# Expert matrices in halves, two experts' loads behind the transposes of gathered rows

## The chip, the cores and the metric

The kernel runs on one core of a Trainium2 chip. A core has a matrix engine (TensorE, PE in the profile), a vector engine (VectorE, DVE), a scalar engine (ScalarE, ACT), GpSimd (POOL) and a sync engine (SyncE, SP) that here only issues transfers. Each engine works through its own instructions in program order, and they wait for each other through semaphores. Transfers run on 16 DMA engines. The metric is the device time of one execution, in microseconds (us), lower is better.

## The reference

The input is x with 8 x 1024 tokens of 256 numbers. A first layer is an attention of each token over its own 16 x 64 numbers, followed by a residual and a normalisation. The second layer is an attention along the first axis (8 positions) for each of 1024 columns, and then a mixture of 8 experts, each with room for 1024 tokens:

```python
slot = jnp.where(keep, idx.astype(jnp.int32) * cap + loc, E * cap)
disp = jnp.zeros((E * cap, D), x.dtype).at[slot].set(xf, mode='drop')
h = jnp.einsum('ecd,edf->ecf', disp, w1) + b1[:, None, :]
y = (jnp.einsum('ecf,efd->ecd', h, w2) + b2[:, None, :]).reshape(E * cap, D)
out = jnp.where(keep[:, None], gate_val[:, None] * y[...], 0.0)
```

There is no nonlinearity between w1 and w2, so an expert is one 256 x 256 matrix w1·w2 and one bias row. The result is normalised, added to the second layer's input, and normalised again.

## The kernel before

**Phases A and B.** phase_a (L120) computes the first layer for 64 tiles of 128 tokens and writes them to DRAM. phase_b (L541) computes the second attention, the normalisation and the gate in 8 groups, and writes a row for each token to rows_d: the normalised value (256), the residual (256) and the gate (1). It also multiplies w1·w2 for experts 0 and 1 (EARLY = 2) and gathers every expert's bias row in acc.

**Phase C** (phase_c, L966) first turns the choice of experts into a list of tokens ordered by expert. VectorE computes each token's slot (L1036 to L1092); then in eight rounds it makes one-hot matrices is_low and is_high (L1111 to L1125), ScalarE makes `both` from is_high (L1127, L1129), and TensorE multiplies them into p_tok (L1139). From p_tok comes `token` (L1150), the indices for the gathers.

Meanwhile TensorE multiplies w1·w2 for experts 2 to 7. expert(e, fc) (L1001) does one of eight pieces of 128 hidden units, with four TensorE records in the trace; the products collect in one PSUM bank pw. After the last piece ScalarE copies the matrix to w12 (L1017), and then load(e + 3) (L995, transfers at L999) issues the next load on SP into one of three buffers. Loads for experts 2, 3 and 4 are issued at the start of the phase (L1027). The function some(k) takes the next k pieces from the list `pieces`; it is called with 8 before the slots are finished (L1052), once in each of the eight rounds (L1146), and with 8 after the token (L1151). So experts 2, 3 and 4 are done when the turns begin.

Then come turns r = -2 to 17 over sixteen batches q of Q = 4 tiles of 128 rows. The list `order` (L1294) is the order of issue in a turn, each entry with its offset of q to r. On GpSimd, gather (L1158) fetches a tile of rows by index, two turns ahead, and scatter (L1278) writes finished rows, two turns behind. turned (L1169) transposes a pair of tiles on TensorE (L1176), ScalarE copies it to xT (L1180), and product (L1183) multiplies it with the expert of the batch, e = q // 2 (L1187, L1197), one turn ahead. some(2) follows: two pieces of experts 5, 6 and 7 a turn, in turns -2 to 1, 2 to 5 and 6 to 9. blend (L1217), roots, scales, normed (L1261) and join (L1270) do both normalisations on VectorE and ScalarE. Expert 5 is needed from batch 10, so in turn 9.

Of the kernel before, what the change touches and what calls it, by code (L numbers as in the profile page):

```python
# [33 lines left out]
P = 128  # L34
# [7 lines left out]
E, FF = 8, 1024  # L42
FC = FF // P
CAP = L * N // E
RW = 2 * D + 1
EARLY = 2
# [4 lines left out]
def fused_kernel(ctx: ExitStack, tc: tile.TileContext, a: dict, out: bass.AP):  # L51
# [38 lines left out]
    nc.scalar.dma_start(keep["gain"], a["ln2_g"].partition_broadcast(P))  # L90
    phase_b(tc, a, ident, x1_d, rows_d, keep, norm_scalars)
    phase_c(tc, a, ident, rows_d, keep, out)


# [871 lines left out]
def phase_c(tc, a, ident, rows_d, keep, out):  # L966


    nc = tc.nc
# [3 lines left out]
    with (  # L973
# [18 lines left out]

        ex = {}

        def load(e):  # L995
            if e < E:
                ex[e] = [xp.tile([P, FC, D], FP, name=n) for n in ("w1", "w2")]
                for tile_, n in zip(ex[e], ("w1T", "w2")):
                    nc.sync.dma_start(tile_, a[n][e].rearrange("(c p) d -> p c d", p=P))  # L999

        def expert(e, fc):  # L1001

            w1, w2 = ex[e]
            if fc == 0:
                ex["w", e] = pw.tile([P, DC * D], FP, name="pw")
            ps = ex["w", e]
            for d in range(DC):
                nc.tensor.matmul(  # L1008
                    ps[:, d * D : (d + 1) * D],
                    w1[:, fc, d * P : (d + 1) * P],  # L1010
                    w2[:, fc, :],
                    start=fc == 0 and d == 0,
                    stop=fc == FC - 1,
                    skip_group_check=True,
                )
            if fc == FC - 1:
                nc.scalar.copy(keep["w12"][:, :, e, :], ps.rearrange("p (c d) -> p c d", c=DC))  # L1017
                load(e + 3)

        pieces = [(e, fc) for e in range(EARLY, E) for fc in range(FC)]  # L1020

        def some(k):
            for _ in range(k):
                if pieces:
                    expert(*pieces.pop(0))

        for e in range(EARLY, EARLY + 3):  # L1027
            load(e)
# [124 lines left out]
        st = {}  # L1153
# [15 lines left out]
        def turned(q, pair):  # L1169

            g = st["g", q]
            pt = pp.tile([P, 512], FP, name="ps")
            for i in range(2):
                for c in range(DC):
                    n = 2 * i + c
                    nc.tensor.transpose(  # L1176
                        pt[:, n * P : (n + 1) * P], g[:, 2 * pair + i, c * P : (c + 1) * P], ident
                    )
            xT = kp.tile([P, 4, P], FP, name="xT")
            nc.scalar.copy(xT, pt)  # L1180
            st["xT", q, pair] = xT

        def product(q, pair):  # L1183
            e = Q * q // ST
            xT = st["xT", q, pair]
            pr = pq.tile([P, 512], FP, name="pr")
            nc.tensor.matmul(  # L1187
                pr.rearrange("p (i d) -> p i d", i=2),
                keep["ones"],
                keep["acc"][:, e, None, :].to_broadcast([P, 2, D]),  # L1190
                start=True,
                stop=False,
                skip_group_check=True,
            )
            for i in range(2):
                for c in range(DC):
                    nc.tensor.matmul(  # L1197
                        pr[:, i * D : (i + 1) * D],
                        xT[:, 2 * i + c, :],
                        keep["w12"][:, c, e, :],  # L1200
                        start=False,
                        stop=c == DC - 1,
                        skip_group_check=True,
                    )
            st["pr", q, pair] = pr
# [72 lines left out]
        def scatter(q, i):  # L1278
# [18 lines left out]
            (gather, -2, 2),  # L1297
            (roots, None),
            (turned, -1, 0),
            (turned, -1, 1),  # L1300
            (product, -1, 0),
            (product, -1, 1),
            (some, None, 2),
            (blend, 0, 0),
            (scales, None),
# [62 lines left out]
```

## Time and profile before

| what | us |
|---|---|
| three timed runs: median (lowest to highest) | 5193.99 (5184.34 to 5194.05) |
| the profiled execution: its own time | 5145.15 |
| its span, from first to last instruction | 5143.4 |
| TensorE busy in it | 4903.2 (95%) |
| phase C, from the slots (L1036) to the end | about 4881 to 5143 |

The profile is of one execution. Its page gives busy time by engine, the span in 40 slices, the DMA queues, the chain of waits that ended last (each piece of work, followed back to what released it), and the costliest groups of instructions. The timeline lists instructions with start and length; in square brackets stands the idle time of the engine just before, and what ended it. "PEld" is the weight load of TensorE, "SPq" an instruction of SP's queue, "granted clock" the share of full speed that TensorE was allowed. A fp32 multiplication shows as two records. L is the line in the kernel.

Some steady rows of phase C: a turn takes about 10.4 us, a gather issue on GpSimd 0.97 us (64 of them), a scatter issue 1.04 us (64).

### The profile page before, as it was taken

How to read it: one execution, taken by the hardware profiler on the slowest of the kernel's cores; microseconds unless marked ns; L12 is line 12 of the kernel's file. 1: busy time of each engine (PE TensorE's matmuls, PEld its weight loads, DVE VectorE, ACT ScalarE, POOL GpSimd, SP SyncE). 2: the span in 40 equal slices, each digit the busy share in tenths (PEclk: the TensorE clock that was granted, in tenths of full speed). 3: DMA queues.
4: the chain of work that ended last, by engine and by line, in shares of the span. 5: the costliest groups of instructions: out<-in, count | busy, mean ns of one | idle time of the engine just before them, and what ended most of it. 6: DMA issues, size and time to landing. Idle time of an engine off the chain costs nothing. (4 is left out here: it accounts for less than half of the span.)

```text
span 5143.4 us, 189684 instructions
## 1 busy us (share of the span) xinstructions
PE 4903.2 (95%) x79688; PEld 3310.9 (64%) x79688; DVE 3070.0 (60%) x6088; ACT 3360.9 (65%) x4123; POOL 3374.4 (66%) x7014
## 2 busy tenths in 40 slices
PE   7999999999999999999999999999999997889675
PEld 4666666666666666666666666666666664566553
DVE  5665655666566666665666656666666563555467
ACT  5777777777777777777777777777777774444234
POOL 5667667677767767766776776776776764254436
PEclk9999999999999999999999999999999998999787
DMA  2222222222222222222222222222222222132253
GB/s 76 47 48 48 48 48 49 47 49 49 46 48 48 47 48 48 49 47 48 49 47 48 49 46 48 48 48 47 48 49 48 49 47 61 48 76 71 66 182 114
DMA packets 575308, 286.29 MB, mean 56 GB/s; under 512 B 394865, under 2 KB 526065, under 8 KB 574449
## 3 DMA queue, kind: packets, MB, share of 16 engines
q1 hardware_dynamic: 365970, 111.51, 10.9%
q0 software_dynamic: 204800, 159.82, 10.4%
q8 instruction: 623, 10.21, 0.8%
q10 hardware_dynamic: 3680, 2.83, 0.2%
q14 instruction: 235, 1.93, 0.1%
HBM read 72.31 MB, written 33.59 MB: 21 GB/s over the span
## 5 line engine op out<-in xcount | busy, mean ns | idle before, releaser
L359 ACT ACTIVATE e<-pair 128x1024 f32<-128x1024 f32 x3072 | 2977.4, 1021 | 1233.0 <-PE pair L343 1233.0
L403 POOL DMA_DIRECT2D nd<-S x4096 | 1952.9, 484 | 613.3 <-DVE S L393 420.9
L343 PE MATMUL pair<-R,L 32*128 32x128 f32 (+1 forms) x32768 | 1605.6, 322 | 2.0 <-POOL event L314 2.0
L393 DVE COPY S<-sum 128x512 f32<-128x512 f32 x1024 | 707.1, 691 | 1465.9 <-PE sum L382 1153.2
L343 PEld LDWEIGHTS pair<-R,L 32*128 32x128 f32 x32768 | 1271.3, 186 | 48.2 <-POOL event L314 2.6
L373 PE MATMUL sum<-e,V 128*32 128x256 f32 x16384 | 1284.9, 385 | 4.9 <-DVE S L393 4.9
L300 POOL DMA_DIRECT2D R<-qm x2048 | 973.8, 483 | 71.7 <-issue 39.2
L382 PE MATMUL sum<-e,V 128*32 128x128 f32 x16384 | 823.3, 273 | 0.0
L382 PEld LDWEIGHTS sum<-e,V 128*32 128x32 f32 x16384 | 532.8, 110 | 352.2 <-issue 0.9
L373 PEld LDWEIGHTS sum<-e,V 128*32 128x32 f32 x16384 | 406.3, 109 | 236.6 <-DVE qm L267 41.8
L331 PE MATMUL pair<-late,sel 32*128 32x256 bf16 (+1 forms) x6144 | 499.3, 313 | 9.6 <-ACT e L359 9.6
L254 DVE COPY V<-vT 32x128 f32<-32x128 f32 x2048 | 457.4, 223 | 28.1
L412 DVE RECIPROCAL att<-nd 128x256 f32<-128x256 f32 x256 | 447.4, 1748 | 8.0 <-DMA nd<-S 4.1
L331 PEld LDWEIGHTS <-sel 32*128 32x128 bf16 x6144 | 155.4, 91 | 460.4 <-issue 445.0
L314 POOL MEMSET event<- 1x1 f32 x256 | 22.8, 89 | 610.9 <-DMA R<-qm 416.4
L234 PEld LDWEIGHTS ps<-xT,wv 128*128 128x128 f32 x2048 | 238.2, 191 | 44.4 <-issue 41.8
L223 PE MATMUL ps<-wk,xT 128*128 128x512 f32 x512 | 255.3, 621 | 10.9 <-DMA wk<-in_Wk 10.1
L234 PE MATMUL ps<-xT,wv 128*128 128x128 f32 x2048 | 262.6, 281 | 1.6 <-DVE qm L267 0.8
L266 PE MATMUL ps<-wq,xT 128*128 128x512 f32 x512 | 255.7, 622 | 6.7 <-DVE k L224 6.7
L443 PE MATMUL ps<-wo,attT 128*128 128x256 f32 x1024 | 257.9, 395 | 0.7 <-ACT attT L426 0.7
L443 PEld LDWEIGHTS ps<-wo,attT 128*128 128x128 f32 x1024 | 186.1, 191 | 63.7 <-issue 41.8
L73 POOL TENSOR_SCALAR ve<-mv 128x1 f32<-128x1 f32 x128 | 37.9, 296 | 271.6 <-DVE mv L71 270.1
(191 smaller groups left out, 3856.0 us busy)
## 6 DMA issues: line engine op xcount, KB each, us to landing
R<-qm POOLq DMA_DIRECT2D x2048, 32.0 KB, 2.1
nd<-S POOLq DMA_DIRECT2D x4096, 16.0 KB, 1.9
L<-k SPq DMA_DIRECT2D x4088, 8.0 KB
rows_d<-yx SPq DMA_DIRECT2D x32, 512.0 KB
xT<-in_xT SPq DMA_DIRECT2D x64, 128.0 KB
xr<-in_x SPq DMA_DIRECT2D x64, 128.0 KB
x_d<-x1o SPq DMA_DIRECT2D x64, 128.0 KB
x<-x_d SPq DMA_DIRECT2D x8, 1024.0 KB
```

What stands on the lines that cost most here:

```text
L234: nc.tensor.matmul(ps[:, i * P : (i + 1) * P], w["v"][:, c, ch * P : (ch + 1) * P], xT_of[t][:, c, :], start=c == 0, stop=c == DC - 1,)
L254: nc.vector.tensor_copy(V[32 * aa : 32 * aa + 32, qd % 2, :, qd // 2, :, aa, 0:4], src[32 * qd : 32 * qd + 32, :, ww, :, aa, :],)
L300: moved.append((None, nc.gpsimd.dma_start(R[:, b, s, b, :], q[:, b, s, cols])))
L331: nc.tensor.matmul(bank[u].rearrange("p (n i) -> p n i", i=n)[:, :, 0:32], sel[pr].rearrange("p a j -> p (a j)"), late[pr, None, :].to_bro ...
L343: one = nc.tensor.matmul(bank[u][:, x * 4 * n : (x + 1) * 4 * n].rearrange("p (b i) -> p b i", i=n), Lt[pr, 2 * (h0 + h) + jb].rearrange(" ...
L359: nc.scalar.activation(e, pair[i], AF.Exp)
L373: nc.tensor.matmul(dst[32 * u : 32 * u + 32], Vs[ww][:, 0, h0 + h, u, :], e0[u // 2][:, u % 2, x * 256 : (x + 1) * 256].rearrange("p (b i) ...
L382: nc.tensor.matmul(dst[32 * u : 32 * u + 32, :, 32:], Vs[ww][:, 1, h0 + h, u, :], e1[u // 2][:, u % 2, h * 128 : (h + 1) * 128].rearrange( ...
L393: nc.vector.tensor_copy(S[:, :, 2 * which : 2 * which + 2, :].rearrange("p b h i -> p h b i"), ps.rearrange("p (h b i) -> p h b i", h=2, b=4),
L403: nc.gpsimd.dma_start(tok[:, b, s, h0 * C1 : (h0 + G) * C1], Sx[:, 4 if s else b, b, :])
L412: nc.vector.reciprocal(att[:, cols], nd[:, 1, cols])
L443: nc.tensor.matmul(ps[:, :D], attT[:, c, :], wo[:, c, :], start=c == 0, stop=c == HID // P - 1)
```

## The change

Loads come in halves: for each half of the hidden units first w1's four chunks, then w2's. For experts 2 to 5 all of an expert's halves are issued together, as before, in four transfers of 512 KB where there were two of 1 MB. Only expert 2's end still issues a load (that of expert 5). The loads of experts 6 and 7, which were issued at the end of experts 3 and 4, are cut into four half loads; load_behind, a new entry of `order` after the products, issues one of them in the turn of q = 0, 2, 4 and 6, and each waits for the last transpose of that batch.

```diff
-        def load(e):
-            if e < E:
+        wait = mybir.DependencyInfo(mybir.DependencyClass.Sync, mybir.DependencyReason.DATA)
+
+        def load(e, halves=(0, 1), behind=None):
+            if 0 in halves:
                 ex[e] = [xp.tile([P, FC, D], FP, name=n) for n in ("w1", "w2")]
-                for tile_, n in zip(ex[e], ("w1T", "w2")):
-                    nc.sync.dma_start(tile_, a[n][e].rearrange("(c p) d -> p c d", p=P))
+            for h in halves:
+                fs = slice(h * FC // 2, (h + 1) * FC // 2)
+                for w, n in zip(ex[e], ("w1T", "w2")):
+                    one = nc.sync.dma_start(w[:, fs, :], a[n][e].rearrange("(c p) d -> p c d", p=P)[:, fs, :])
+                    if behind is not None:
+                        tc.add_manual_dep(one.ins, behind.ins.name, wait, reason="transfers in turn with the rows")
+
+
+        halves = [(e, h) for e in range(EARLY + 4, E) for h in range(2)]
+
+        def load_behind(q):
+            if q % 2 == 0 and halves:
+                e, h = halves.pop(0)
+                load(e, (h,), st["turned", q])
...
-                load(e + 3)
+                if e == EARLY:
+                    load(e + 3)
...
-                    nc.tensor.transpose(
+                    last = nc.tensor.transpose(
...
             st["xT", q, pair] = xT
+            st["turned", q] = last
...
             (product, -1, 1),
+            (load_behind, -1),
             (some, None, 2),
```

## The prediction, on record before the result

> **What bounds the kernel now.** I read the page first. TensorE is busy for 95% of the span, nearly all of it in phases A and B, which the diff leaves alone. So only the last stretch can move: phase C, from about 4880 us to 5143.4. I then read the chain of waits from 4870 us.
>
> ```profile
> 4879.81 6.17 DMA rows_d<-gate
> 4886.32 0.37 SPq L999
> 4886.74 7.96 DMA w<-in_w
> 4894.70 0.38 issue
> 4895.08 10.00 PE pw L1008 x32
> 4905.58 0.73 ACT both L1127
> 4906.36 1.10 PE pr L1139 x8
> 4907.48 1.22 DVE is_low L991
> ...
> 4925.11 7.11 DMA g<-rows_d,token
> 4932.26 0.44 PE ps L1176 x2
> 4932.70 0.86 PE pr L1187 x2
> ```
>
> Each row is start, length, what. Two transfers stand in the chain. The first is the matrices of expert 2: TensorE cannot begin L1008 until both whole matrices are there, and VectorE's one-hot batches (L991) come behind that expert. The second is a gather of rows that lands 7.11 us after its issue began, with weights moving beside it. The timeline by instruction shows how much of each is waiting:
>
> ```profile
> 4889.60 0.63 PE L1051 MATMUL ps<-over,ones 128*128 128x64 f32 x2
> 4895.08 9.99 PE L1008 MATMUL pw<-w,w 128*128 128x256 f32 x32 [4.84 <-DMA w<-in_w]
> 4907.48 1.22 DVE L991 TENSOR_TENSOR is_low<-low,column 128x1024 bf16<-128x1024 f32 x1 [5.77 <-PE pr L1139]
> 4928.31 0.37 SPq L999 DMA_DIRECT2D w<-in_w1T  x1
> 4930.79 1.01 PE L1176 MATMUL ps<-ident,g 128*128 128x128 f32 x6
> 4931.36 0.20 PEld L1176 LDWEIGHTS ps<-ident,g 128*128 128x128 f32 x2 [0.20 <-DMA g<-rows_d,token]
> 4932.26 0.20 PEld L1176 LDWEIGHTS ps<-ident,g 128*128 128x128 f32 x2 [0.70 <-DMA g<-rows_d,token]
> ```
>
> TensorE waits 4.84 us for expert 2, VectorE 5.77 us for TensorE behind it. For the first gathered rows TensorE waits only 0.20 + 0.70 us, because up to 4930.8 it was still multiplying for experts 4 and 5. From 4932.3 to 4955.1 it runs without a wait.
>
> **Part 1: loads in halves.** load() now sends four transfers of 512 KB per expert where it sent two of 1 MB, the first halves of both matrices in front. This touches experts 2, 3, 4 (issued together) and 5, so eight more transfers in all. The first pieces of expert 2 need 1.05 MB instead of 2.10. The DMA view in steps of 1 us gives what had moved: 0.11 MB by 4888, 0.41 by 4889, 0.77 by 4890, 1.11 by 4891, 1.48 by 4892, and 2.44 by 4894.70, when the 2.10 MB were there (0.34 MB of the next transfer ran beside them). So 1.05 MB have moved at 4890.8 at the earliest; with the same 0.34 MB ahead (1.39 MB) it is 4891.76. I take the later, nearest to the measured landing, and add the 0.38 us issue row: L1008 starts at 4892.1 instead of 4895.08, 2.9 us earlier. The ends are 3.9 (nothing runs ahead) and 0 (TensorE still waits for the whole tile; the edit would then do nothing here). The second half should land near 4894.7 as now, while TensorE needs sixteen records first: no second wait.
>
> The 32 records take 10.0 us because the clock is half at first:
>
> ```profile
> 4895.00:4897.00 2.00, 1.92 (x5) 0.50 1.10 349
> 4899.00:4901.00 2.00, 2.00 (x6) 0.54 1.11 350
> 4901.00:4903.00 2.00, 2.00 (x11) 1.00 1.13 353
> ```
>
> Columns: stretch, length, TensorE busy (records), granted clock, DMA share, GB/s. The step to 1.00 comes about 5.8 us after the start. The same 32 records at full clock (4921.11) take 7.17 us, 0.224 each; so 13 ran slowly at 0.44 here. If 5.8 slow microseconds follow the new start too, the expert ends at 4892.1 + 10.0 = 4902.1, and the gain stays 2.9. [...] I keep 2.9, from the row.
>
> That gain reaches the token. VectorE has three one-hot batches ready at 4901.7 and then stands until 4907.48; at 4904.6 it still stands, so it takes up the whole 2.9. After it VectorE runs five rounds of 2.06 us with no wait, and the token, the first gather (4921.14) and TensorE's expert 4 (4921.11) follow together.
>
> [...] I cost the extra issues at nothing; what hides them is that the queue stays full, and SP (0.37 to 0.58 us for an issue that isn't held back) has nothing else to do.
>
> **Part 2: experts 6 and 7 move.** Removed: the four 1 MB loads issued at 4920.47, 4920.88, 4928.31 and 4928.73, which fill the DMA engines until about 4947, beside the first gathers. Those land in 7.1 us (median, 4920 to 4930) against 3.6 over the whole phase. At 3.6 the fourth gather, issued at 4925.11 - 2.9 = 4922.2, lands at 4925.8, before TensorE is free at 4930.8 - 2.9 = 4927.9. So the 0.20 + 0.70 = 0.9 us wait goes, and nothing more: what is late next is TensorE itself, with expert 4 in front of the transposes. Bounds: 0 if the gathers stay slow, and 0.9.
>
> Added: four pairs of half transfers (two DMA issues each), behind the last transposes of q = 0, 2, 4, 6. Only SP waits, and behind it on SP stand only the next halves and the end of the kernel. The buffers are long free (experts 3 and 4 are finished). Use comes late: expert 6's halves go out in turns r = -1 and 1 and are read from r = 2 and 4; expert 7's in 3 and 5, read from 6 and 8. A turn is 7.8 us at the start (TensorE) and 10.4 later, so each has over 15 us for some 4 to 7 us.
>
> Each half pair (1.05 MB at 350 GB/s, 3.0 us) meets gathers. In r = -1 there are over 10 us until those rows are turned; in r = 1 GpSimd has stopped gathering and stands until the first scatter (24.3 us idle). For r = 3 and 5, in the times of before:
>
> ```profile
> 4974.14 0.44 PE L1176 MATMUL ps<-ident,g 128*128 128x128 f32 x2 [0.98 <-DMA g<-rows_d,token]
> 4981.16 0.97 POOL L1162 DMA_INDIRECT g<-rows_d,token  x1 [0.30 <-issue]
> 4984.49 0.44 PE L1176 MATMUL ps<-ident,g 128*128 128x128 f32 x2 [1.74 <-DMA g<-rows_d,token]
> 5005.62 1.36 POOL L1283 DMA_INDIRECT out<-o,token  x1 [5.32 <-ACT o L1265]
> ```
>
> The half behind the transposes of 4974.14 moves from about 4976 to 4979. The gather that TensorE waits for next is issued at 4981.16, after it. In r = 5 the half moves from 4996.5 to 5000, and then GpSimd stands 5.3 us before the next deciding gather. I cost both at 0; the other end is 3.5 us each (7.1 - 3.6), 7.0 together, or 14.0 if all four cost it. A gain from them is excluded: nothing there waits for weights.
>
> **Sum.** -2.9 - 0.9 = -3.8 us: span 5143.4 becomes about 5139.6, the profiled time 5145.15 about 5141.3. The three timed runs are about 1% above the profiled one (median 5193.99), from work that the change leaves alone, so I carry the difference over: 5193.99 - 3.8 = 5190.2. The bounds of the mechanism: -5.0 (4.1 + 0.9) to +11.1 (-2.9 + 14.0, the 0.9 kept as it is). The three runs spread over 9.7 us, 0.19%; a difference within 0.2% (10.4 us) is about what measurement here cannot tell from none.
>
> **The rivals.**
> *No gain (0.20).* The halves help nothing, because the wait stays with whole tiles or six more transfers slow the first, and the early loads were covered anyway. For it: only 0.9 us of the gathers' slowness was ever waited for. Against it: L1008's pieces read only their own half. Between 0 and 0.9 saved: 5193.5.
> *More than the sum (0.13).* TensorE reaches full clock sooner and the quieter queues shorten the start-up beyond what I read, where GpSimd waits 24.3 us and VectorE 9.5. Against it: both hang on TensorE's unbroken work. A gain over 0.2% would need 10.4 us, twice my bound; 5182 would be such a result.
> *Slower (0.07).* The halves land on the loop gather, transposes, product, weights copy, norm, which has no slack in r = 5 (VectorE waits 5.4 us for it). Price 3.5 us per half. From the second half that costs it, the gain is gone; with all four, and the first gathers as slow as now, 5193.99 + 11.1 = 5205.1.
> *The sum as worked out (0.60):* 5190.2.
>
> **How the numbers follow.** Faster: 0.13 of the second rival, and 0.06 of the two cases near zero, since one of three runs sat 9.7 us under the median. Slower: 0.04 of the third rival (that with all four halves), and 0.02 for the spread. The rest, 0.75, is within 0.2%. The range is 5179 to 5198: below, the largest gain less the spread (5189 - 9.7); above, no gain and some 4 us, under half the spread.
>
> **What would show it.** Right: L1008's first wait shrinks from 4.84 to about 1.9 us, VectorE's 5.77 to about 2.9, the token and first gather come at about 4918.2, gathers there land in under 5 us, the 0.90 us before L1176 is gone, and the turns after it stay at 10.4 us. Wrong: L1008 starts at 4895 still; a second wait between its halves; gathers in r = 3 or 5 that hold TensorE beyond its 1.7 us; or a wait for w in a turn from r = 2 on. The prediction fails if phases A and B move by more than the 3.8 us at stake.

## The result and the profile after

| | median us (lowest to highest), runs | before, beside it | ratio, 95% interval |
|---|---|---|---|
| the change, first series | 5189.82 (5184.73 to 5195.04), 20 | 5191.43, 20 runs | 0.9997 [0.9991, 1.0004] |
| the change, second series | 5185.85 (5184.06 to 5191.25), 13 | 5190.71, 17 runs | 0.9992 [0.9984, 1.0001] |

The first series is the result: no difference that these runs can tell, between -4.7 and +2.1 us. The means of all runs of both series (33 and 37) differ by -2.7 us. Forecast were -3.8 us and 5190.2. Kernels are only compared with the kernel before on their own chip, because on one chip, used for three experiments below, the kernel before takes 5148.8 us.

The timeline of the changed kernel has these lines for the places shown before. (L1022 was L1008, L1154 was L1139, L1191 was L1176, L1195 and L1242 were L1180 and L1226, the copy to xT and the blend; L1213 was L1197, the product.)

```profile
4892.31 0.63 PE L1066 MATMUL ps<-over,ones 128*128 128x64 f32 x2
4894.69 9.95 PE L1022 MATMUL pw<-w,w 128*128 128x256 f32 x32 [1.75 <-DMA w<-in_w]
4907.06 1.23 DVE L991 TENSOR_TENSOR is_low<-low,column 128x1024 bf16<-128x1024 f32 x1 [2.64 <-PE pr L1154]
4930.15 1.01 PEld L1191 LDWEIGHTS ps<-ident,g 128*128 128x128 f32 x8
4930.37 1.04 PE L1191 MATMUL ps<-ident,g 128*128 128x128 f32 x8
4934.31 0.59 ACT L1195 COPY xT<-ps 128x512 f32<-128x512 f32 x1 [2.72 <-PE pr L1213]
4944.92 0.48 DVE L1242 SCALAR_TENSOR_TENSOR z<-pr,gate,g 128x256 f32<-128x256 f32 x1 [16.21 <-remote]
4947.95 1.07 ACT L1195 COPY xT<-ps 128x512 f32<-128x512 f32 x2 [13.05 <-remote]
```

The first three rows are the forecast's Part 1: 1.75 us of wait where 4.84 were, 2.64 where 5.77 were. The next two are its Part 2: eight transposes in one row and no wait for rows. The last three are new: ScalarE's second copy waits 2.72 us. VectorE's first blend waits 16 us for something with no recorded releaser ("remote"), ScalarE's next copy 13 us, though the transposes that it copies ended by 4939.5.

I call such waits holds. They are not the change's: the kernel before, profiled once more, has them too. The first two rows are its wait for expert 2, the third is its first blend, late as well, and the last two are held:

```profile
4898.03 9.96 PE L1008 MATMUL pw<-w,w 128*128 128x256 f32 x32 [4.40 <-DMA w<-in_w]
4910.41 1.23 DVE L991 TENSOR_TENSOR is_low<-low,column 128x1024 bf16<-128x1024 f32 x1 [5.30 <-PE pr L1139]
4943.84 0.48 DVE L1226 SCALAR_TENSOR_TENSOR z<-pr,gate,g 128x256 f32<-128x256 f32 x1 [8.22 <-PE ps L1176]
4950.93 0.48 DVE L1226 SCALAR_TENSOR_TENSOR z<-pr,gate,g 128x256 f32<-128x256 f32 x1 [4.88 <-remote]
4951.05 1.07 ACT L1180 COPY xT<-ps 128x512 f32<-128x512 f32 x2 [14.61 <-remote]
```

The chain of waits of phase C names them as "another core or an unknown queue", first in that second profile of before, then in the changed kernel:

```profile
4936.44 14.59 another core or an unknown queue
4996.07 8.21 another core or an unknown queue
5039.39 8.19 another core or an unknown queue
5066.13 8.29 another core or an unknown queue
5102.53 7.41 another core or an unknown queue
```

```profile
4934.89 13.03 another core or an unknown queue
4992.83 8.43 another core or an unknown queue
5036.20 8.33 another core or an unknown queue
5063.09 8.57 another core or an unknown queue
5099.46 8.29 another core or an unknown queue
```

The five sum to 46.7 us each time, and the chain of the first profile of before has no such row. Phase C (from the issue of the gate's store to the end) took 263.6 us in that first profile and 306.7 in the second: these 43 us are most of the 1% between the profiled execution and the timed runs that the prediction carried over.

Single executions of one program begin phase C up to 3 us apart (4879.81 and 4882.81 for before), so all profiles are compared from the issue of the gate's store. Times in us; the last three columns count from the first gather:

| profile | expert 2 starts | token | first gather | store to end | first blend | first scatter | end |
|---|---|---|---|---|---|---|---|
| before, first | 15.27 | 40.07 | 41.33 | 263.6 | 14.2 | 48.0 | 222.3 |
| before, again (holds) | 15.22 | 40.01 | 41.28 | 306.7 | 19.8 | 57.3 | 265.5 |
| changed (holds) | 12.40 | 37.17 | 38.45 | 305.0 | 24.2 | 57.4 | 266.6 |
| changed, again (holds) | 12.11 | 36.73 | 38.01 | 304.3 | 25.5 | 57.3 | 266.3 |
| halves alone | 12.46 | 37.23 | 38.49 | 260.8 | 14.3 | 48.2 | 222.3 |
| changed, gathers in turn | 12.73 | 37.10 | 38.36 | 259.7 | 13.3 | 47.1 | 221.3 |
| changed, expert 3 first | 18.56 | 41.99 | 43.25 | 266.4 | 13.3 | 47.1 | 223.1 |

What follows finds out which part of the gain arrives where.

### The profile page after: what moved, and what is told of

Read it like the earlier page. It is cut to its first block, busy times and chain, and to the rows that moved or that the text cites. A ratio compares the mean times of both kernels' runs of the same rounds, so it can differ in the third digit from the quotient of the medians.

```text
span 5187.3 us, 189704 instructions
## 1 busy us (share of the span) xinstructions
PE 4912.9 (95%) x79688; PEld 3314.9 (64%) x79688; DVE 3070.8 (59%) x6088; ACT 3360.4 (65%) x4123; POOL 3376.7 (65%) x7014
## 5 line engine op out<-in xcount | busy, mean ns | idle before, releaser
L443 PE MATMUL ps<-wo,attT 128*128 128x256 f32 x1024 | 257.8, 395 | 0.7 <-ACT attT L426 0.7
```

The costliest lines, as they stand in the source:

```text
L443: nc.tensor.matmul(ps[:, :D], attT[:, c, :], wo[:, c, :], start=c == 0, stop=c == HID // P - 1)
```

## The experiments

**Are the holds the change's doing?** The kernel before, unchanged.

> The kernel before, unchanged, profiled a second time. The profile of the change shows five waits of some 8 us in the turns (ScalarE's xT copy waits for transposes whose records ended long before), 40 us in all, and the profile of before shows none, though the two medians differ by 1.6 us. Theory A (the waits belong to the program as it usually runs): they stand in this profile too, its span is near 5189, and phase C from the gate's store to the end takes about 305 us. Theory B (the moved loads cause them, and the rest of the program is quicker by as much): none here, phase C about 264 us, and the span near 5189 only if phases A and B are 40 us longer than in the first profile.

5191.26 us, with the five holds shown above. They come without the moved loads too, and on three of the four chips that the experiments ran on; theory B falls.

**Phase C behind a short phase B.** Phase A is left out of three kernels, x is copied to its result, so that less noise lies ahead of phase C:

```diff
-    phase_a(tc, a, ident, x1_d, norm_scalars)
+    (x copied to x1_d, eight tiles of 128 rows at a time)
```

The third one has all loads in halves, but none moved:

```diff
-                if e == EARLY:
+                if e + 3 < E:
                     load(e + 3)
...
-            (load_behind, -1),
```

> The kernel before without phase A: x is copied to where the first layer's result would be, so the first layer is left out. Span some 590 to 650 us, in which a few us of phase C are 0.5% and can be timed. This is the base for the next two. Theory A: waits of some 8 us in the turns here too.

> The changed kernel, first layer left out as in the short kernel before. My sum: 3.8 us less than the short kernel before (5.0 at most, 1.6 at least). Rival 'no gain': within 1 us of it. Theory B (moved loads cause 8 us waits): 10 to 40 us more than it.

> Only the halves: experts 6 and 7 are loaded where they were, in halves like the others; first layer left out. My sum: 2.9 us less than the short kernel before, 0.9 more than the short changed kernel. Rival 'no gain': equal to the short kernel before. Theory B: quicker than the short changed kernel by 10 us or more.

Medians of five: 915.68, 915.74 and 915.24 us, each with runs 3.2 to 6.6 us apart; the time itself I had put far too low, because phase B and the copy take some 610 us. The medians tell nothing, the profiles do. Expert 2's row in the timeline of before, changed and halves alone (L1013 and L1027 are its line in these kernels):

```profile
630.82 10.14 PE L1013 MATMUL pw<-w,w 128*128 128x256 f32 x32 [5.07 <-DMA w<-in_w]
```

```profile
630.28 9.89 PE L1027 MATMUL pw<-w,w 128*128 128x256 f32 x32 [2.17 <-DMA w<-in_w]
```

```profile
629.75 10.12 PE L1027 MATMUL pw<-w,w 128*128 128x256 f32 x32 [1.57 <-DMA w<-in_w]
```

From the store, the token comes at 40.85, 37.71 and 37.33 us, the end at 300.1, 296.7 and 296.4, and from first gather to end it is 257.9, 257.7 and 257.8. All three have the holds. So in these single profiles the halves' 3.1 to 3.5 us reach the end of phase C whole (3.4 and 3.7 there), and the moved loads add and cost nothing (257.7 against 257.8).

**Phase C alone.** Phases A and B are left out; rows are copied from x, token p goes to expert p mod 8, and the matrices of experts 0 and 1 and the bias rows are zero. Four orders of loads: before, changed, halves alone (diff above), moved alone (experts 2 to 5 whole).

> Phase C of the kernel before alone: phases A and B are left out, the rows are copied from x, and token p of a tile goes to expert p mod 8, so every expert has its 1024 rows. With no work ahead that varies, a few us of phase C should be timed to about 1 us. This is the base for the next three. Span some 480 to 560 us; 8 us waits for transposes in the turns as in the repeated profile of before.

> Phase C of the changed kernel alone, the same parts left out. My sum: 3.8 us less than phase C of before alone (2.9 of it before the token, 0.9 at the first transposes). Rival 'no gain', now in a sharper form: the token comes 2.8 us earlier, as the profiles have it, but the turns give it back, so the two are within 1 us. Rival 'slower': the halves that move inside the turns cost up to 3.5 us each, and it is longer than with halves alone by 3 us or more.

> Phase C alone with the halves alone: experts 6 and 7 in halves at their old places. My sum: 2.9 us less than phase C of before alone, and 0.9 more than that of the change. If the turns give the gain back whatever the loads do: equal to before. If only the moved loads give it back: 2.9 us less than before and less than the change.

> Phase C alone with the move alone: experts 2 to 5 in whole matrices, 6 and 7 in halves behind the transposes. My sum: 0.9 us less than phase C of before alone. If moved loads cost something in the turns: longer than before by some us. The token's place is that of before in either case.

Medians of five: 478.77, 480.58, 479.51 and 481.25 us, each with runs 3.7 to 6.2 us apart. The halves can't help here: expert 2's weights came before they were wanted, and in all four its product starts 5.6 us after the same instruction of VectorE (the comparison `upto`). By the medians the moved loads would cost 1.1 us with halves (changed against halves alone) and 2.5 with whole matrices (moved alone against before); in the profiles, first gather to end is 258.6, 258.2, 259.7 and 260.1, so the moved loads there make -1.5 and +1.5. That is inconclusive, and it led me to expect 2 to 3 us in the next kernel, wrongly.

**The halves alone, in the whole kernel** (the second diff above). This and the next two ran together on the chip where the kernel before takes 5148.82 us (33 runs) and no profile has a hold.

> The whole kernel with one part of the change alone: every expert's matrices in halves, but the loads of experts 6 and 7 where they were before (behind an expert's product). Prediction's theory: the 2.9 us at L1008 are there (expert 2's product starts 12.4 us after the gate's store instead of 15.2, the token list at 37.2 instead of 40.0), and the time is 5188.5 (5191.4 less 2.9). Theory 2 (the moved loads cost some 2 to 3 us in the turns, as the timings of phase C alone had it): this kernel is 2 to 3 us below the changed one, 5187. Theory 3 (the turns swallow whatever the front gains): 5191, equal to before, with the token list still at 37.2. In the profile the stretch from the first gather to the end is the sum's test: 265.5 us in the repeated profile of before and 266.6 in the changed kernel; theory 2 wants 263 to 264 here, the others 265.5 to 266.6.

5145.98 us (13 runs), ratio 0.9995 [0.9987, 1.0004]. The prediction's theory holds for the halves: expert 2 at 12.46, token at 37.23, first gather to end 222.3 as in the first profile of before. Its timeline still has the waits for rows that Part 2 was to remove:

```profile
4894.22 9.95 PE L1022 MATMUL pw<-w,w 128*128 128x256 f32 x32 [1.76 <-DMA w<-in_w]
4906.59 1.23 DVE L991 TENSOR_TENSOR is_low<-low,column 128x1024 bf16<-128x1024 f32 x1 [2.65 <-PE pr L1154]
4930.61 0.20 PEld L1191 LDWEIGHTS ps<-ident,g 128*128 128x128 f32 x2 [0.35 <-DMA g<-rows_d,token]
4931.51 0.20 PEld L1191 LDWEIGHTS ps<-ident,g 128*128 128x128 f32 x2 [0.70 <-DMA g<-rows_d,token]
4934.57 0.48 DVE L1242 SCALAR_TENSOR_TENSOR z<-pr,gate,g 128x256 f32<-128x256 f32 x1 [2.82 <-PE pr L1213]
```

**Fewer gathers ahead of the first turn.** The first gathers of batches 2, 3 and 4 each wait for the first blend of the batch two earlier, so that 8 gathers and not 19 stand ahead of the first transposes. Cut to its core:

```diff
+            if i == 0 and 2 <= q <= 4:
+                tc.add_manual_dep(one.ins, st["first z", q - 2].ins.name, wait, reason="gathers in turn with the blends")
...
-            (gather, -2, 0),
-            (gather, -2, 1),
-            (gather, -2, 2),
...
             (blend, 0, 0),
+            (gather, -2, 0),
+            (gather, -2, 1),
+            (gather, -2, 2),
```

> The changed kernel, with the gathers of the batches 2 to 4 each waiting for the first blend (z) of the batch two earlier, so that 8 gathers stand ahead of the first transposes instead of 19. It tests what holds ScalarE's copy of the transposed rows (xT) in the first turn until 27.0 us after the first gather, in every profile but the first one of before, though the transposes' own records end by 19.3. Theory H (the release waits until the run of gathers has drained: 19 gathers end at 26.9): with 8 gathers, which drain by some 15 to 17, the third copy of xT comes at 16 to 19 us after the first gather instead of 27.0, the second batch's blend at 20 to 24 instead of 31.3, and if the later turns keep their rhythm the end comes 5 to 10 us earlier, 5180 to 5185. Theory I (the hold has nothing to do with the gathers: it is fixed in the program's order or in time): third xT still at 27, and the time 5190, or 2 to 6 us more, since a gather now is late for its transposes. Theory J (the hold goes, but the gathers held back land late): third xT early, end 5188 to 5195.

5143.26 us (13 runs), ratio 0.9992 [0.9983, 1.0000]. The test of theory H failed to come about: on this chip nothing is held, with 19 gathers ahead or with 8. But the kernel contains the whole change, and so shows it with no hold (L1193, L1197, L1244 and L1215 are here the transposes, the copy, the blend and the product):

```profile
4928.34 1.01 PEld L1193 LDWEIGHTS ps<-ident,g 128*128 128x128 f32 x8
4928.56 1.04 PE L1193 MATMUL ps<-ident,g 128*128 128x128 f32 x8
4929.19 1.07 ACT L1197 COPY xT<-ps 128x512 f32<-128x512 f32 x2 [2.52 <-PE ps L1193]
4932.22 0.48 DVE L1244 SCALAR_TENSOR_TENSOR z<-pr,gate,g 128x256 f32<-128x256 f32 x1 [5.37 <-PE pr L1215]
4936.97 1.07 ACT L1197 COPY xT<-ps 128x512 f32<-128x512 f32 x2 [6.70 <-PE ps L1193]
```

The waits for rows are gone, for the reason forecast: the gathers land sooner. The view of transfers from 4917 to 4931 (number of gathers issued, median us to landing) has first the halves alone, with weights still moving there, then this kernel:

```profile
g<-rows_d,token POOLq DMA_INDIRECT x9, 6.9
g<-rows_d,token POOLq DMA_INDIRECT x8, 3.8
```

In the next kernel, whose gathers stand in the old order, ten of them land in 3.9. The first blend comes 3.66 us after these transposes began, where the halves alone need 4.67 (from 4929.90 to 4934.57). The 1.0 us stays to the end: first scatter 47.1 against 48.2, end 221.3 against 222.3. Store to end is 259.7, 3.9 below the first profile of before. The slower gathers themselves add nothing: the next kernel, without them, has the same 13.3 and 47.1.

**The dose: expert 3's matrices ahead of expert 2's.** This lengthens the wait for expert 2, to see how much of the delay arrives.

```diff
-        for e in range(EARLY, EARLY + 3):
+        for e in (EARLY + 1, EARLY, EARLY + 2):
             load(e)
```

> The changed kernel with the two matrices of expert 3 (four halves) issued ahead of those of expert 2: a dose of the same wait, with the other sign and four times as large. PE's first product of phase C then waits for two more megabytes: at 5.8 us a matrix, 11.6 us later. Theory A (the start of that product passes whole to the token list and through the turns to the end): product at 24.0 us after the gate's store instead of 12.4, token at 48.8 instead of 37.2, time 5201.4 (5189.8 plus 11.6). Theory B (the holds in the turns take up part of what happens ahead of them): the token list is late by 11.6, but the time rises by 0 to 8 us only. A rise of less than 10 us in the stretch to the token list would say that part of the wait lies beside VectorE's own work.

5150.36 us (12 runs), ratio 1.0003 [0.9994, 1.0011]. I had the dose wrong: 5.8 us is what both matrices of an expert take (2.10 MB; SP's issues of 512 KB, held back, stand 1.46 us apart in this kernel from 4895.32 to 4899.70, and four of them are 5.84), not one, so the delay should be 5.8. The product starts 6.1 us later than with the halves alone (18.56 - 12.46), the token only 4.8. The 1.3 us between are in the product's own length (the wait before it stands without a named releaser, as "issue"):

```profile
4902.83 8.61 PE L1022 MATMUL pw<-w,w 128*128 128x256 f32 x32 [7.88 <-issue]
```

It takes 8.6 us instead of 9.95. The table by stretch of 2 us (TensorE busy with records, weight loads, VectorE, ScalarE, GpSimd, granted clock, DMA share, GB/s) shows why, for this kernel and then for the halves alone:

```profile
4902.00:4904.00 2.00, 1.17 (x3) 1.02 (x4) 1.99 (x3) 0.00 (x0) 0.00 (x0) 0.50 1.10 348
4904.00:4906.00 2.00, 2.00 (x7) 1.61 (x6) 1.97 (x4) 0.00 (x0) 0.00 (x0) 0.55 1.11 350
4906.00:4908.00 2.00, 2.00 (x11) 1.77 (x10) 0.40 (x2) 0.00 (x0) 0.00 (x0) 1.00 1.10 347
```

```profile
4894.00:4896.00 2.00, 1.78 (x4) 1.52 (x5) 1.86 (x5) 0.00 (x0) 0.00 (x0) 0.50 1.10 349
4896.00:4898.00 2.00, 2.00 (x6) 1.58 (x5) 1.79 (x9) 0.00 (x0) 0.00 (x0) 0.50 1.10 347
4898.00:4900.00 2.00, 2.00 (x6) 1.56 (x6) 1.97 (x4) 0.00 (x0) 0.00 (x0) 0.52 1.10 349
4900.00:4902.00 2.00, 2.00 (x11) 1.77 (x10) 1.97 (x4) 0.00 (x0) 0.00 (x0) 1.00 1.11 350
```

Half clock lasted 3.0 us after this product's start, 5.7 after the other's. Less these 1.3 us, the delay passes to the token whole (theory A). Later this kernel loses 1.7 us in turn r = 5, in products that take 3.41 us instead of 1.89. First this kernel, then the one with gathers in turn, each with the last wait for rows and the products behind it:

```profile
5000.43 0.44 PE L1193 MATMUL ps<-ident,g 128*128 128x128 f32 x2 [1.81 <-DMA g<-rows_d,token]
5001.74 3.41 PE L1215 MATMUL pr<-w,xT 128*128 128x256 f32 x8
```

```profile
4991.85 0.44 PE L1193 MATMUL ps<-ident,g 128*128 128x128 f32 x2 [1.65 <-DMA g<-rows_d,token]
4992.98 1.89 PE L1215 MATMUL pr<-w,xT 128*128 128x256 f32 x8
```

The rows land at the same time after the first gather (72.9 us both); the clock fell in one (0.50 granted from 5002 to 5004) and stayed at 1.00 in the other. It isn't the moved half that comes there: both kernels have it, 73.4 us after the first gather.

**The changed kernel again.**

> The changed kernel unchanged. In the last three kernels the holds of 8 us were absent (the kernel before took 5148.8 us beside them, as in its first profile), and two of them, which hold both parts of the change, had the first blend 13.3 us after the first gather instead of 14.2: the 0.9 us of Part 2 that the changed kernel's own profile did not show. One of them also lost 1.7 us later, at the turn in which a moved half of expert 7 came just ahead of a gather (PE waited 8.0 us for rows instead of 6.5, and the clock fell). If the holds are absent here too: first blend at 13.3, token at 37.2 after the gate's store, the stretch from first gather to end 221.4 (the 0.9 kept, nothing lost later; ratio to before about 0.9993) or 223.1 (1.7 lost again; ratio about 0.9996, the change then no better than the halves alone at 0.9995). If the holds are there: first blend at 20 to 24, that stretch 265 to 267, ratio 0.9995 to 0.9999, and the 0.9 is again not to be seen.

5185.85 us (second series above). It ran on a chip with the holds: first blend at 25.5, first gather to end 266.3, and the 0.9 us not to be seen. (Its expectation put expert 3's loss of 1.7 us down to rows that came late; by the rows just shown it was the clock.)

## Why the prediction was right, and where not

*Part 1, 2.9 us: right, in size and in path.* Expert 2 starts 2.8 us earlier (12.40 against 15.22) and the token comes 2.84 earlier (37.17 against 40.01) in the changed kernel, 3.3 in its second profile, and 2.84 with the halves alone. Without holds the whole of it is at the end: phase C 260.8 against 263.6, the medians 2.84 apart (with an interval of -6.7 to +2.1, so the trace carries this, not the timing). That the product kept its length (9.95 us) was luck: the prediction took 5.8 us of half clock to follow the new start, and 5.7 did, but with gathers in turn the product took 9.55 us and with expert 3 first 8.61, after 3.0 us of half clock. No run shows the 4.1 us that the bound of -5.0, and with it the range's lower end, has for this part: with the halves in their own order the token came 2.8 to 3.3 us earlier in the whole kernels and 3.1 and 3.5 in the short ones, and a product as short as 8.61 us was seen only behind a start 6.1 us later. The extra transfers at no cost are right too: TensorE waits for no weights after its first 1.75 us, and the halves alone, with twelve more transfers than before, lose nothing (222.3 us from first gather to end in both). Their queue moves 347 to 362 GB/s in every stretch of some 2 us from 4892 to 4904; the first profile of before has 337 to 372 in every microsecond from 4889 to 4895.

*Part 2's gain of 0.9 us at the first transposes: right about the wait, wrong about the time where there are holds.* The wait is gone in both profiles of the change. Without holds, 0.9 to 1.0 us arrive at the end. With them it is lost, and more: the first blend comes 24.2 and 25.5 us after the first gather where before has 19.8, but the next copy to xT comes at 27.2 and 27.1 where before has 27.0. That copy's release, not TensorE, sets the second batch, and the first scatter is at 57.3 to 57.4 in all three. Between first gather and end the change then stands 0.8 to 1.1 us worse than before (266.3 and 266.6 against 265.5), a difference between single profiles. So there the sum fails in its second term: -2.8 with nothing behind it and about 1 us given back, instead of -3.8.

*Moved loads at no cost in the turns: right without holds, open with them.* From first scatter to the start of the last it is 164.2 us before, 164.1 with the halves alone and 164.1 with gathers in turn. With holds it is 198.1 before, but 199.1 and 199.0 in the two profiles of the changed kernel: the 0.8 to 1.1 us lie here. The short kernels, with holds too, show no such loss, and the halves alone ran with holds only there and in phase C alone, so whether the moved loads cost it isn't shown. The rival that had them slow the loop in r = 5 (3.5 us per half) did not occur; a loss at that very place did, 1.7 us, and was the clock's.

*The carry-over of 1%: right number, wrong reason.* The prediction took the difference between the profiled and the timed runs to come "from work that the change leaves alone". Most of it comes from holds in phase C, on the path that the change is about. The sum still held, because the holds are as long in both kernels; but a term of that sum was costed in a profile that had none.

*The sum.* Without holds, phase C with the whole change is 3.9 us shorter, against a forecast of 3.8. With holds it is 1.7 and 2.4 shorter in the profiles (305.0 and 304.3 against 306.7), and 2.7 by the means of all timed runs. No kernel here beats the others by more than its interval: the changed kernel with its gathers in turn is at 0.9992 [0.9983, 1.0000]. So the timed runs alone exclude neither the sum nor the rival of no gain; the parts are told apart by the traces. And that 5189.82 came so near to 5190.2 is luck: the three runs of before gave a base 2.6 us too high (5193.99, where twenty give 5191.43), and the medians then moved by 1.6 us, not 3.8.

## What to carry to other kernels

Cutting the first transfer so that its consumer can begin on half of it was worth about half that transfer here (2.84 us of 5.8); that this holds elsewhere, where the path from there is unbroken, is my estimate from this one case. Read the gain at a milestone of the trace (here the token, which came at 36.7 to 37.2 us in the four profiles that should agree), and not from medians whose interval is 7 us wide. A wait that goes is worth nothing where the next release downstream is set by something else (here 0.9 us of wait, with a copy to xT that came at 27.2 and 27.1 us against 27.0): follow the chain until the milestone after it. And where one profiled execution is 1% from the timed runs, profile the same kernel again before placing that 1% anywhere.

## What the runs showed of the hardware

- Holds of about 8 us (7.4 to 8.6, and a first one of 13 to 15) in phase C, five to an execution (and one of 1.5 more in the changed kernel's second profile), in every whole-kernel profile but those of one chip and the first of before. ScalarE or VectorE stands though TensorE's records have ended; the third copy to xT comes 27.0 to 27.2 us after the first gather, just as the first run of 19 gathers has drained (in the changed kernel the transfers stop at 4946.7 and the copy starts at 4947.95), whatever loads move beside it; without holds it comes at 18.9 in the first profile of before and at 18.1 with gathers in turn. With the holds, records of landings are missing: 12,347 to 12,423 of 12,544 on each of the eight semaphores of GpSimd's transfers in the first profile of the changed kernel; without holds, 12,543 or 12,544 in the first profile of before. All that are missing in the changed kernel fall behind the first gather: of 2048 there, 760 are recorded, and 2048 in that profile of before. The view of transfers has no time to landing for the 64 gathers in the changed kernel and in the second profile of before, where the first has 3.6 us. So the holds may belong to the recording, which is not shown: every timed run here has a span and a clock on record, and none shows the kernel with nothing recorded. What holds the release stays open: no run with the holds had fewer gathers ahead.
- The clock's step to full speed does not count from the product's start: it came 5.7 us after it with the halves alone, and 3.0 with expert 3 first, whose product started 6.1 us later. In the first profile of before the granted clock changes between 1.00 and 0.50 after stretches of 3.41, 13.65, 61.44, 6.83, 37.55, 6.83, 40.96 and 6.83 us, from 4883.77 to 5061.26: each is a multiple of the shortest within 0.01 us (3.413, and 61.44 is eighteen of them). An order of loads moved 1.3 us one way (8.61 us for the product against 9.95) and 1.7 us the other (from products of 3.41 us against 1.89) in places where the clock differed.
